# Two graph attention layers on one core: norms split by token tile, weigh placed ahead of scores, probability scalings on ScalarE

## The chip, the cores and the metric

The kernel runs on one core of a Trainium2 chip. A core has five engines that matter here, each with a queue of its own: TensorE (PE) multiplies matrices, VectorE (DVE) and ScalarE (ACT) work element by element and can read PSUM, GpSimd (POOL) works element by element in SBUF, and SyncE (SP) issues transfers. The metric is device time in microseconds (us) of one execution. Three runs of the kernel before took 3923.49 to 3931.69 us, with a median of 3928.25.

## The reference

There are 64 graphs of 256 nodes with 512 features, and a boolean adjacency matrix for each. Two layers follow each other; all arithmetic is in fp32.

```
# layer 0, 4 heads of 64
h = relu(layernorm(x))
q, k, v = h @ Wq, h @ Wk, h @ Wv
p = softmax(where(adj, q k^T / 8, -max))
x = x + (p v) @ Wo + bo
# layer 1, 8 heads of 64, adjacency with the diagonal added
h = relu(layernorm(x))
h = layernorm(h) * gamma + beta
q, k, v = split(h @ w_qkv.T)
p = softmax(where(adj | eye, q k^T / 8, -1e9))
x = x + (p v) @ w_out.T + b_out
```

## The kernel before

One step (index s) handles two graphs, which are four tiles (t) of 128 tokens; there are 32 steps. A step passes through these functions:

- load_h brings x and the adjacency matrix in. norm0 takes mean and variance of each token tile on DVE (moments: L198, L199), the inverse root on POOL (L203, a power of -0.5 over all four tiles at once) and scales the rows on DVE (scale_rows, L208, one instruction a tile).
- transpose_h turns the normalised rows so that features lie on partitions (PE L252, four transposes a call, four calls c a layer), and copies them out of PSUM: on ACT for layer 0 (L256, with the relu), on DVE for layer 1 (L258, with gamma and beta). After the fourth call POOL forms sums of them (act_sums, L96 to L99).
- project_qk and project_v multiply by the weights (PE L325 and L347), combine multiplies by the output weights (PE L362). All three use a scheme of Strassen and Winograd: seven products instead of eight, called in the order 1, 6, 7, 5, 2, 4, 3. Products 2, 4 and 3 go on in the PSUM banks of products 1, 7 and 5, so these banks stay taken until late. Each product is taken out by ACT or DVE: evacuate (L269 to L281) for the projections, accumulate (L288 to L303) for combine. In accumulate, product 1 is copied to u by ACT (L288), and product 6 is added to u by DVE (L290).
- scores handles a pair of heads (pr) for both graphs: PE L386; then eight blocks of 128 x 256, in two groups of four, one for each graph g. In a group and for each of four blocks, DVE adds the mask and takes the extreme value (L396), and ACT takes the exponential with its sum (L402). After the four, DVE forms the reciprocals of the sums (L407), and the four blocks are scaled by them: those of the first head of the pair (e == 0) on DVE (L412), those of the second on ACT (L414).
- turn transposes the probabilities (PE L423) and copies them back, by DVE for the first head (L427) and by ACT for the second (L429).
- weigh multiplies them by v (PE L441); ACT copies the result into oT (L447), and after the last pair POOL forms its sums (act_sums).
- norm1 prepares layer 1: for each token tile moments, subtraction of the mean with relu (DVE L231), moments again and the addition of the output bias on POOL (L235). After the fourth tile come the variance terms (L237, L238), the inverse root on POOL (L203) and four L208.
- mask makes the additive mask from the adjacency bytes on POOL (L188; for layer 1 also two L192). The mask of layer 1 has one buffer, so a new one can only be written when the last scores of the step before have read the old one.

PSUM is split in two pools of four banks each: ps_sc for scores and turn, ps_mm for everything else.

Which work stands where is decided by a list of places. A step lasts 6 units of place, and what belongs to layer 0 of step s runs in the period two before that of its layer 1. So layer 0 of one step fills the gaps of layer 1 of another. The calls are sorted by place and made in that order:

```python
    def at(period, place, fn, *args):
        events.append((period * PERIOD + place * SET, len(events), fn, args))
```

PE keeps the order of the calls exactly (manual_schedule at L59). On the other engines the framework's scheduler orders the instructions when the program is built, with its own estimate of when each will be ready. When they run, each engine takes its queue in order. The buffers of a pool are given out when the program is built, too.

In the steady state, the part of a period that the following sections speak of runs like this on PE: scores of layer 1, pair 1; product 1 of combine of layer 0 (another step); weigh of pair 2; two transposes of layer 0 (L252); product 6 of combine; two more transposes; the other five products of combine; turn of pair 1; products 1 and 6 of project_qk of layer 0; scores of pair 3; weigh of pair 1; products 7, 5, 2 and 4 of project_qk; turn of pair 3; product 3.

Of the kernel before, what the change touches and what calls it, by code (L numbers as in the profile page):

```python
# [8 lines left out]
FP = mybir.dt.float32  # L9
U8 = mybir.dt.uint8  # L10
AF = mybir.ActivationFunctionType
ALU = mybir.AluOpType

EPS = 1e-5
# [5 lines left out]
def kernel(  # L20
# [16 lines left out]
    nc = tc.nc  # L37
    P = 128
    B, N, D = x.shape
# [4 lines left out]
    NT = G * NIC  # L44
# [9 lines left out]
    act = ctx.enter_context(tc.tile_pool(name="act", bufs=1))  # L54
    sm = ctx.enter_context(tc.tile_pool(name="sm", bufs=2))
    stat = ctx.enter_context(tc.tile_pool(name="stat", bufs=4))
# [52 lines left out]
    bout_b = const.tile([P, D], FP, name="bout_b")  # L109
# [57 lines left out]
    S = [dict() for _ in range(NSTEP)]  # L167
# [28 lines left out]
    def moments(mv, src, t):  # L196
        bs = stat.tile([P, 6], FP, name="bs")
        nc.vector.bn_stats(bs, src[:, t, :])  # L198
        nc.vector.bn_aggr(mv[:, t, :], bs)  # L199

    def rsqrt(var, name):
        r = stat.tile([P, NT], FP, name=name, bufs=2)
        nc.gpsimd.tensor_tensor(r, var, mhalf, ALU.pow)  # L203
        return r

    def scale_rows(h, mean, r):
        for t in range(NT):
            nc.vector.tensor_scalar(  # L208
                h[:, t, :], h[:, t, :], mean[:, t, 0:1], r[:, t:t + 1],
                op0=ALU.subtract, op1=ALU.mult,  # L210
            )

    def norm0(s):
        h = S[s]["h"]
        mv = stat.tile([P, NT, 2], FP, name="mv0", bufs=2)
        for t in range(NT):
            moments(mv, h, t)
        ve = stat.tile([P, NT], FP, name="ve0", bufs=2)
        nc.vector.tensor_scalar(ve, mv[:, :, 1], EPS, None, op0=ALU.add)
        scale_rows(h, mv, rsqrt(ve, "r0"))  # L220

    def norm1(s):
        st, x1 = S[s], S[s]["xt"]
        mv = stat.tile([P, NT, 2], FP, name="mv1", bufs=2)
        mg = stat.tile([P, NT, 2], FP, name="mg", bufs=2)
        h = st["h"] = act.tile([P, NT, D], FP, name="h")
        for t in range(NT):
            moments(mv, x1, t)  # L230
            nc.vector.tensor_scalar(  # L231
                h[:, t, :], x1[:, t, :], mv[:, t, 0:1], 0.0, op0=ALU.subtract, op1=ALU.max
            )
            moments(mg, h, t)
            nc.gpsimd.tensor_tensor(x1[:, t, :], x1[:, t, :], bout_b, ALU.add)  # L235
        ve = stat.tile([P, NT], FP, name="ve1", bufs=2)
        nc.vector.tensor_scalar(ve, mv[:, :, 1], EPS, EPS, op0=ALU.add, op1=ALU.mult)  # L237
        nc.vector.tensor_tensor(ve, ve, mg[:, :, 1], ALU.add)  # L238
        scale_rows(h, mg, rsqrt(ve, "r1"))


    def blocks_of(b, pairs):
# [134 lines left out]
    def scores(s, lyr, pr):  # L377
        st = S[s]
        qk, neg = st.pop(("qk", lyr, pr)), st[f"n{lyr}"]
        sc = {h: ps_sc.tile([P, NIC, N], FP, name="sc") for h in HEADS}  # L380
        for g in range(G):
            for ic in range(NIC):
                for e in range(2):
                    rows = slice(e * DH, (e + 1) * DH)
                    i0 = g * N + ic * P
                    nc.tensor.matmul(  # L386
                        sc[g, e][:, ic, :], qk[rows, 0, i0:i0 + P],
                        qk[rows, 1, g * N:(g + 1) * N], start=True, stop=True,
                    )
        pm = {h: sm.tile([P, NIC, N], FP, name="pm", bufs=8) for h in HEADS}  # L390
        sa = stat.tile([P, 3, G, 2, NIC], FP, name="sa", bufs=2)
        for g in range(G):
            for e in range(2):
                for ic in range(NIC):

                    nc.vector.tensor_tensor_reduce(  # L396
                        out=pm[g, e][:, ic, :], in0=sc[g, e][:, ic, :],
                        in1=neg[:, g * NIC + ic, :],
                        scale=-SCALE, scalar=SMAX, op0=ALU.add, op1=ALU.min,
                        accum_out=sa[:, 0, g, e, ic:ic + 1],  # L400
                    )
                    nc.scalar.activation(  # L402
                        pm[g, e][:, ic, :], pm[g, e][:, ic, :], AF.Exp,
                        bias=sa[:, 0, g, e, ic:ic + 1], scale=-1.0,
                        accum_out=sa[:, 1, g, e, ic:ic + 1],
                    )
            nc.vector.reciprocal(sa[:, 2, g], sa[:, 1, g])  # L407
            for e in range(2):
                for ic in range(NIC):
                    pv, inv = pm[g, e][:, ic, :], sa[:, 2, g, e, ic:ic + 1]  # L410
                    if e == 0:
                        nc.vector.tensor_scalar(pv, pv, inv, None, op0=ALU.mult)  # L412
                    else:
                        nc.scalar.activation(pv, pv, AF.Copy, scale=inv)  # L414
        st["pm", lyr, pr] = pm

    def turn(s, lyr, pr):
# [42 lines left out]
    def at(period, place, fn, *args):  # L460
        events.append((period * PERIOD + place * SET, len(events), fn, args))

    def at_set(period, place, share, fn, *args):
        for i, n in enumerate((1, 6, 7, 5, 2, 4, 3)):
            at(period, place + i * share / 7, fn, *args, n)

    for s in range(NSTEP):

        p = s - 2
        at(p - 1, 5.6, load_h, s)  # L470
        at(p, 1.0, norm0, s)
        at(p, 2.9, mask, s, 0)
        for c in range(NC):
            at(p, 3.03 + 0.03 * c, transpose_h, s, 0, c)
        at_set(p, 3.5, 1.0, project_qk, s, 0, 0)
        at_set(p, 4.5, 0.5, project_v, s, 0)
        at(p, 4.5, scores, s, 0, 0)
        at(p, 5.15, turn, s, 0, 0)
        at(p, 5.6, scores, s, 0, 1)
        at(p, 5.601, weigh, s, 0, 0, True, False)  # L480
        at(p, 6.3, turn, s, 0, 1)
        at(p, 7.001, weigh, s, 0, 1, False, True)
        at(p, 7.4, load_x, s)
        at(p, 8.6, first_bias, s)
        at_set(p, 9.0, 0.5, combine, s, 0)
        at(p, 9.5, norm1, s)

        p = s
        for c in range(NC):
            at(p, -0.85 + 0.15 * c, transpose_h, s, 1, c)  # L490
        at(p, 0.3, mask, s, 1)
        at_set(p, 0.0, 1.0, project_qk, s, 1, 0)
        at_set(p, 1.0, 1.0, project_v, s, 1)
        at_set(p, 2.0, 1.0, project_qk, s, 1, 1)
        at(p, 1.0, scores, s, 1, 0)
        at(p, 1.65, turn, s, 1, 0)
        at(p, 2.0, scores, s, 1, 2)
        at(p, 2.001, weigh, s, 1, 0, True, False)
        at(p, 2.65, turn, s, 1, 2)
        at(p, 3.0, scores, s, 1, 1)  # L500
        at(p, 3.001, weigh, s, 1, 2, False, False)
        at(p, 3.5, turn, s, 1, 1)
        at(p, 3.75, scores, s, 1, 3)
        at(p, 3.751, weigh, s, 1, 1, False, False)
        at(p, 4.25, turn, s, 1, 3)
        at(p, 4.501, weigh, s, 1, 3, False, True)
        at_set(p, 5.0, 1.0, combine, s, 1)
        at(p, 6.0, store, s)

# [38 lines left out]
```

## Time and profile before

| | |
|---|---|
| median of three runs | 3928.25 us |
| profiled execution | 3926.11 us |
| its span, first to last instruction | 3924.3 us |
| mean granted clock of PE | 0.978 |
| PE busy | 3665.1 us, 93% |
| DVE busy | 2517.4 us, 64% |
| ACT busy | 1690.2 us, 43% |
| POOL busy | 1385.1 us, 35% |
| L412, scaling on DVE | 768 instructions, 354.6 us, mean 501 ns |
| L414, scaling on ACT | 768 instructions, 345.6 us, mean 498 ns |
| L402, exponential on ACT | 1536 instructions, 760.9 us, mean 496 ns |
| L396, masking on DVE | 1536 instructions, 563.1 us, mean 416 ns |

A row of the groups names line, engine and operation, then what is written from what, and how often; behind it stand the busy time, the mean duration, and the idle time of the engine just before, with what ended it. Durations overlap: the next instruction of a kind may start before the one before it has ended, so the pitch from start to start can be shorter than the mean. PE's matmuls in fp32 appear as two records each. A busy share says little about the end of the kernel, except for the engine that is nearly always busy; for the others the waits tell which of their results came late.

### The profile page before, as it was taken

The numbers are of one execution on the slowest core, as the hardware profiler recorded it, in microseconds if no ns is written. First come the engines' busy times: TensorE is split into PE (matmuls) and PEld (weight loads), VectorE is DVE, ScalarE is ACT, GpSimd is POOL, SyncE is SP. The second block draws the span as 40 slices with busy tenths as digits, with TensorE's granted clock in tenths as the row PEclk, the third lists the DMA queues.
The fourth block names the chain that finished last, engine by engine and source line by source line (L and its number), as shares of the span: only waits on it lengthen the run. The fifth ranks groups of instructions, "written<-read, shape, count | busy, mean of one in ns | idle before, by whom it ended". The sixth has DMA issues, their size and how long they took to land.

```text
span 3924.3 us, 59006 instructions
## 1 busy us (share of the span) xinstructions
PE 3665.1 (93%) x21953; PEld 3039.7 (77%) x21953; DVE 2517.4 (64%) x7193; ACT 1690.2 (43%) x4945; POOL 1385.1 (35%) x1170
## 2 busy tenths in 40 slices
PE   5999999999999999999999999999999999999988
PEld 4787778877778877788777878777887778787767
DVE  5666666666666666656666666666566666666654
ACT  2444444444444344444444443444444444444443
POOL 4244333343332433333433324333334333243331
PEclk9999999999999999999999999999999999999999
DMA  3000000010000100100000001101010000010000
GB/s 118 12 34 34 6 31 33 34 35 21 16 33 34 34 34 2 34 33 34 34 13 24 33 34 34 34 2 34 33 35 34 13 24 33 35 34 33 1 22 22
DMA packets 74127, 115.45 MB, mean 29 GB/s; under 512 B 18792, under 2 KB 22384, under 8 KB 73840
## 3 DMA queue, kind: packets, MB, share of 16 engines
q1 hardware_dynamic: 67584, 104.87, 7.8%
q10 hardware_dynamic: 6256, 6.82, 0.6%
q8 instruction: 172, 2.82, 0.3%
q14 instruction: 115, 0.94, 0.1%
HBM read 78.12 MB, written 33.55 MB: 28 GB/s over the span
## 4 chain that ended last, share of the span: by engine, by line
PE 70%; DVE 16%; ACT 9%; POOL 2%; issue 2%; DMA 1%; ACTq 0%; DVEq 0%; POOLq 0%
PE mm L325 23%; PE mm L362 14%; PE mm L347 13%; PE sc L423 7%; PE sc L386 7%; ACT pm L402 6%; PE mm L441 5%; DVE bs L198 4%; DVE pm L396 3%; PE mm L252 3%; ACT pm L414 2%; DVE h L231 2%; DVE pm L412 2%; DVE h L208 2%; DVE pm L427 1%
## 5 line engine op out<-in xcount | busy, mean ns | idle before, releaser
L325 PE MATMUL mm<-hT,wqkv 128*128 128x256 f32 x5376 | 1236.8, 385 | 112.9 <-DVE qk L273 100.0
L325 PEld LDWEIGHTS mm<-hT,wqkv 128*128 128x128 f32 x5376 | 1015.2, 192 | 281.8 <-issue 138.5
L402 ACT ACTIVATE pm<-pm,sa 128x256 f32<-128x256 f32 x1536 | 760.9, 496 | 706.1 <-DVE sa L396 701.9
L362 PE MATMUL mm<-wo,oT 128*128 128x256 f32 x2688 | 655.0, 393 | 91.4 <-ACT oT L447 72.2
L396 DVE CUSTOM_DVE_ANT_0 pm<-sc,n 128x256 f32<-128x256 f32 x1536 | 563.1, 416 | 188.5 <-PE sc L386 186.0
L362 PEld LDWEIGHTS mm<-wo,oT 128*128 128x128 f32 x2688 | 503.7, 196 | 187.3 <-issue 91.3
L347 PE MATMUL mm<-wqkv,hT 128*128 128x128 f32 (+1 forms) x3584 | 627.7, 330 | 6.8 <-DVE v L273 4.7
L347 PEld LDWEIGHTS mm<-wqkv,hT 128*128 128x128 f32 x3584 | 545.2, 191 | 81.7 <-issue 24.5
L291 POOL TENSOR_TENSOR xt<-xt,u 128x512 f32<-128x512 f32 x64 | 81.3, 1271 | 1120.2 <-DVE u L290 1120.2
L429 ACT COPY pm<-sc 128x512 f32<-128x512 f32 x384 | 225.1, 586 | 505.2 <-PE sc L423 505.2
L423 PE MATMUL sc<-ident,pm 128*128 128x128 f32 x3072 | 385.4, 279 | 17.8 <-DVE pm L412 17.7
L423 PEld LDWEIGHTS sc<-ident,pm 128*128 128x128 f32 x3072 | 360.3, 145 | 43.2 <-DVE pm L412 23.7
L386 PE MATMUL sc<-qk 64*128 64x256 f32 x3072 | 384.0, 389 | 1.0 <-DVE qk L281 1.0
L441 PE MATMUL mm<-pm,v 128*64 128x256 f32 x3072 | 376.3, 387 | 0.0
L414 ACT ACTIVATE pm<-pm,sa 128x256 f32<-128x256 f32 x768 | 345.6, 498 | 58.5 <-DVE sa L407 58.5
L412 DVE TENSOR_SCALAR pm<-pm,sa 128x256 f32<-128x256 f32 x768 | 354.6, 501 | 5.8
L386 PEld LDWEIGHTS sc<-qk 64*128 64x128 f32 x3072 | 278.6, 186 | 80.7 <-issue 47.1
L427 DVE COPY pm<-sc 128x512 f32<-128x512 f32 x384 | 254.3, 685 | 116.3 <-PE sc L423 116.1
L441 PEld LDWEIGHTS mm<-pm,v 128*64 128x64 f32 x3072 | 204.4, 137 | 147.4 <-issue 54.9
L402 ACT ACTIVATION_READ_ACCUMULATOR pm<-pm,sa 128x1 f32 x1536 | 287.3, 187 | 0.0
L96 POOL TENSOR_TENSOR oT<-oT 128x512 f32<-128x512 f32 (+1 forms) x64 | 73.8, 1154 | 557.9 <-ACT oT L447 557.9
L184 POOL TENSOR_TENSOR xt<-xt,bo_b 128x512 f32<-128x512 f32 x128 | 161.5, 1292 | 254.8 <-DMA xt<-in_x_dram 254.8
(78 smaller groups left out, 3427.6 us busy)
## 6 DMA issues: line engine op xcount, KB each, us to landing
h<-in_x_dram SPq DMA_DIRECT2D x32, 1024.0 KB, 5.2
xt<-in_x_dram SPq DMA_DIRECT2D x32, 1024.0 KB, 5.1
out_dram<-xt SPq DMA_DIRECT2D x32, 1024.0 KB, 4.3
ad<-in_adj_dram SPq DMA_DIRECT2D x32, 128.0 KB, 2.2
wr<-in_L_gnn_w_qkv_dram ACTq DMA_DIRECT2D x3, 1024.0 KB, 8.7
wr<-in_L_gnn_w_out_dram ACTq DMA_DIRECT2D x1, 1024.0 KB, 9.6
wqkv<-in_L_gnn_Wq_dram ACTq DMA_DIRECT2D x4, 128.0 KB, 5.0
wqkv<-in_L_gnn_Wk_dram ACTq DMA_DIRECT2D x4, 128.0 KB, 4.1
```

What stands on the lines that cost most here:

```text
L325: nc.tensor.matmul(bank[:, k, :], w[:, wa, c, k, a * P:(a + 1) * P], st["hT"][:, ba, c, :], start=first and (k, c) == (0, 0), stop=(k, c) ...
L347: nc.tensor.matmul(bank[:, t, :], st["hT"][:, ba, c, t * P:(t + 1) * P], w[:, wa, c, 2, :], start=first and (t, c) == (0, 0), stop=(t, c) ...
L362: nc.tensor.matmul(bank[:, t, :], st[f"oT{lyr}"][:, ba, c, t * P:(t + 1) * P], w[:, wa, c, :], start=first and (t, c) == (0, 0), stop=(t, ...
L386: nc.tensor.matmul(sc[g, e][:, ic, :], qk[rows, 0, i0:i0 + P], qk[rows, 1, g * N:(g + 1) * N], start=True, stop=True,)
L396: nc.vector.tensor_tensor_reduce(out=pm[g, e][:, ic, :], in0=sc[g, e][:, ic, :], in1=neg[:, g * NIC + ic, :], scale=-SCALE, scalar=SMAX, o ...
L402: nc.scalar.activation(pm[g, e][:, ic, :], pm[g, e][:, ic, :], AF.Exp, bias=sa[:, 0, g, e, ic:ic + 1], scale=-1.0, accum_out=sa[:, 1, g, e ...
L412: nc.vector.tensor_scalar(pv, pv, inv, None, op0=ALU.mult)
L414: nc.scalar.activation(pv, pv, AF.Copy, scale=inv)
L423: nc.tensor.transpose(pp[:, jc, ic * P:(ic + 1) * P], pm[:, ic, jc * P:(jc + 1) * P], ident)
L427: nc.vector.tensor_copy(pm, pp)
L429: nc.scalar.copy(pm, pp)
L441: nc.tensor.matmul(po[e * DH:(e + 1) * DH, g, :], st[f"v{lyr}"][:, g * NIC + jc, c0:c0 + DH], pT[g, e][:, jc, :], start=(jc == 0), stop=(j ...
```

## The change

Three things change.

Norms come in pieces. scale_rows becomes scale_row, which handles one tile. norm0 and norm1 become functions of one tile, too; the call for the last tile also makes the variance terms and the inverse root. Each piece has a place of its own. norm0 stood at place 1.0 whole; its pieces stand at 0.4 to 1.6, and its scalings at 2.05 to 2.65. norm1 stood at 9.5 whole; its pieces stand at 9.5 to 10.25, its scalings at 10.5 to 10.8. The operations and their number are the same.

weigh is placed 0.001 ahead of the scores of the next unit, where it stood 0.001 behind them.

All scalings of probabilities run on ACT.

```diff
-    def scale_rows(h, mean, r):
-        for t in range(NT):
-            nc.vector.tensor_scalar(
-                h[:, t, :], h[:, t, :], mean[:, t, 0:1], r[:, t:t + 1],
-                op0=ALU.subtract, op1=ALU.mult,
-            )
+    def scale_row(s, t):
+        h, mean, r = S[s]["h"], S[s]["mean"], S[s]["r"]
+        nc.vector.tensor_scalar(
+            h[:, t, :], h[:, t, :], mean[:, t, 0:1], r[:, t:t + 1],
+            op0=ALU.subtract, op1=ALU.mult,
+        )
...
+    def norm1(s, t):
         st, x1 = S[s], S[s]["xt"]
...
+        moments(mv, x1, t)
+        nc.vector.tensor_scalar(
+            h[:, t, :], x1[:, t, :], mv[:, t, 0:1], 0.0, op0=ALU.subtract, op1=ALU.max
+        )
+        moments(mg, h, t)
+        nc.gpsimd.tensor_tensor(x1[:, t, :], x1[:, t, :], bout_b, ALU.add)
+        if t == NT - 1:
+            ve = stat.tile([P, NT], FP, name="ve1", bufs=2)
+            nc.vector.tensor_scalar(ve, mv[:, :, 1], EPS, EPS, op0=ALU.add, op1=ALU.mult)
+            nc.vector.tensor_tensor(ve, ve, mg[:, :, 1], ALU.add)
+            st["r"] = rsqrt(ve, "r1")
...
                     pv, inv = pm[g, e][:, ic, :], sa[:, 2, g, e, ic:ic + 1]
-                    if e == 0:
-                        nc.vector.tensor_scalar(pv, pv, inv, None, op0=ALU.mult)
-                    else:
-                        nc.scalar.activation(pv, pv, AF.Copy, scale=inv)
+                    nc.scalar.activation(pv, pv, AF.Copy, scale=inv)
...
-        at(p, 1.0, norm0, s)
+        for t in range(NT):
+            at(p, 0.4 + 0.4 * t, norm0, s, t)
+            at(p, 2.05 + 0.2 * t, scale_row, s, t)
...
-        at(p, 5.601, weigh, s, 0, 0, True, False)
+        at(p, 5.599, weigh, s, 0, 0, True, False)
...
-        at(p, 7.001, weigh, s, 0, 1, False, True)
+        at(p, 6.999, weigh, s, 0, 1, False, True)
...
-        at(p, 9.5, norm1, s)
+        for t in range(NT):
+            at(p, 9.5 + 0.25 * t, norm1, s, t)
+            at(p, 10.5 + 0.1 * t, scale_row, s, t)
...
-        at(p, 2.001, weigh, s, 1, 0, True, False)
+        at(p, 1.999, weigh, s, 1, 0, True, False)
...
-        at(p, 3.001, weigh, s, 1, 2, False, False)
+        at(p, 2.999, weigh, s, 1, 2, False, False)
...
-        at(p, 3.751, weigh, s, 1, 1, False, False)
+        at(p, 3.749, weigh, s, 1, 1, False, False)
...
-        at(p, 4.501, weigh, s, 1, 3, False, True)
+        at(p, 4.499, weigh, s, 1, 3, False, True)
```

The instructions of the built program can be listed engine by engine for both kernels. With the lines of the kernel before, around the part described above, they stand like this (ACT after the scores of pair 1, and POOL between the sums of hT and those of oT):

```
        before                                  changed
ACT     6 L402, 2 L414, 2 L402, L288,           L447, 6 L402, 4 L414, 2 L402,
        2 L414, L447, 4 L256                    L288, 4 L414, 4 L256
POOL    4 L235, L203, L188, 2 L192              3 L235, L188, L235, 2 L192, L203
```

On DVE, before, the maskings L396 of pair 3 are mixed with rows 2 and 3 of norm1. In the changed kernel all eight stand together behind three rows, ahead of the end of row 3, the copy L273, the variance terms and the four L208; the second reciprocal L407 stands behind the first L208.

More of the change, by code (lines that the diff above doesn't have):

```diff
@@ L204, in rsqrt @@
         return r
-    def scale_rows(h, mean, r):
-        for t in range(NT):
-            nc.vector.tensor_scalar(
-                h[:, t, :], h[:, t, :], mean[:, t, 0:1], r[:, t:t + 1],
-                op0=ALU.subtract, op1=ALU.mult,
-            )
[L213 to L220, printed above, removed]
@@ L224, in norm1 @@
-    def norm1(s):
-        st, x1 = S[s], S[s]["xt"]
[L226 to L239, printed above, removed]
+    def scale_row(s, t):
[4 more added lines that the diff above has]
+        )
@@ new lines, in norm0 @@
+    def norm0(s, t):
+        st = S[s]
+        if t == 0:
+            st["mean"] = stat.tile([P, NT, 2], FP, name="mv0", bufs=2)
+        moments(st["mean"], st["h"], t)
+        if t == NT - 1:
+            ve = stat.tile([P, NT], FP, name="ve0", bufs=2)
+            nc.vector.tensor_scalar(ve, st["mean"][:, :, 1], EPS, None, op0=ALU.add)
+            st["r"] = rsqrt(ve, "r0")
+    def norm1(s, t):
+        st, x1 = S[s], S[s]["xt"]
+        if t == 0:
+            st["mv"] = stat.tile([P, NT, 2], FP, name="mv1", bufs=2)
+            st["mean"] = stat.tile([P, NT, 2], FP, name="mg", bufs=2)
+            st["h"] = act.tile([P, NT, D], FP, name="h")
+        mv, mg, h = st["mv"], st["mean"], st["h"]
+        moments(mv, x1, t)
[4 more added lines that the diff above has]
+        nc.gpsimd.tensor_tensor(x1[:, t, :], x1[:, t, :], bout_b, ALU.add)
+        if t == NT - 1:
+            ve = stat.tile([P, NT], FP, name="ve1", bufs=2)
+            nc.vector.tensor_scalar(ve, mv[:, :, 1], EPS, EPS, op0=ALU.add, op1=ALU.mult)
+            nc.vector.tensor_tensor(ve, ve, mg[:, :, 1], ALU.add)
+            st["r"] = rsqrt(ve, "r1")
```

## The prediction

> **What bounds the kernel now.** I read the page first: TensorE (PE) is busy 93% of the span, VectorE (DVE) 64%, ScalarE (ACT) 43%, GpSimd (POOL) 35%. So only what makes PE idle, or slow, is worth anything. The waits of PE alone come next; the columns are total us, times, longest.
>
> ```profile
> PE mm L325 <- DVE qk L273: 100.0, 30, 3.6
> PE mm L362 <- ACT oT L447: 72.2, 30, 2.4
> PE mm L252 <- DVE h L208: 21.6, 3, 17.5
> PE mm L362 <- POOL oT L98: 17.8, 3, 12.2
> PE sc L423 <- DVE pm L412: 17.7, 21, 4.5
> ```
>
> Two waits come once in each of 30 steps: stall Q (3.3 us, in project_qk of layer 0) and stall C (2.4 us, in combine of layer 0). The rest belongs to start and end. From one stall C to the next it is 119.97 us on average ((3671.41 - 192.27) / 29, timeline). Then the windows view around one stall C; the seventh figure, behind the five engines, is the granted clock.
>
> ```profile
> 2112.50:2115.00 2.50, 0.09 (x2) 0.06 (x1) 0.79 (x3) 2.50 (x8) 0.00 (x0) 1.00 0.00 0
> 2115.00:2118.00 3.00, 3.00 (x10) 2.52 (x11) 0.69 (x1) 0.90 (x3) 0.12 (x1) 0.50 0.02 5
> ```
>
> After the stall PE runs at half clock for about 3.4 us and loses 1.7 us more. Taking a window of 12 us around each stall, 19 of 30 C and 16 of 30 Q show it: some 2.0 us per step. Without stalls a step would be 119.97 - 2.4 - 3.5 - 2.0 = 112.0 us (3.5 is Q with the 0.27 us that the turn behind it waits).
>
> What ends stall C is in ACT's timeline (start, us, operation), with PE's last:
>
> ```profile
> 2110.70 0.50 ACT L402 ACTIVATE pm<-pm,sa 128x256 f32<-128x256 f32 x1
> 2111.20 0.90 ACT L414 ACTIVATE pm<-pm,sa 128x256 f32<-128x256 f32 x2
> 2112.98 0.57 ACT L288 COPY u<-mm 128x512 f32<-128x512 f32 x1
> 2113.44 0.91 ACT L414 ACTIVATE pm<-pm,sa 128x256 f32<-128x256 f32 x2
> 2114.25 0.57 ACT L447 COPY oT<-mm 128x512 f32<-128x512 f32 x1
> 2114.72 1.08 ACT L256 ACTIVATE hT<-mm 128x512 f32<-128x512 f32 x2
> ...
> 2114.97 2.04 PE L362 MATMUL mm<-wo,oT 128*128 128x256 f32 x4 [2.41 <-ACT oT L447]
> ```
>
> The second product of combine needs a PSUM bank of ps_mm (four of them). The one it gets was filled by weigh, whose copy L447 stands behind a whole softmax unit in ACT's queue: exps at a pitch of 0.49 us, scalings at 0.40 (two take 2111.20 to 2111.99). Note L256 right behind: the copies of the transposes free the next two banks. Stall Q, in the same way, from DVE, PE and POOL:
>
> ```profile
> 2017.69 1.91 DVE L208 TENSOR_SCALAR h<-h,mg,r 128x512 f32<-128x512 f32 x4 [0.91 <-POOL r L203]
> 2020.20 0.69 DVE L273 TENSOR_TENSOR qk<-mm,qk 128x512 f32<-128x512 f32 x1
> ...
> 2021.04 1.97 PE L325 MATMUL mm<-hT,wqkv 128*128 128x256 f32 x8 [3.48 <-DVE qk L273]
> ...
> 2016.60 1.06 POOL L203 TENSOR_TENSOR r<-ve,mhalf 128x4 f32<-128x4 f32 x1 [0.55 <-DVE ve L238]
> 2020.38 1.04 POOL L188 TENSOR_SCALAR n<-ad 128x1024 f32<-128x1024 uint8 x1 [2.72 <-DVE sa L396]
> 2021.51 2.55 POOL L192 TENSOR_TENSOR n<-n,offdiag 128x512 f32<-128x512 f32 x2
> ```
>
> The copy L273 waits in DVE's queue behind norm1; the inverse root L203 runs ahead of the mask (L188, L192), which has to wait for the last masking L396 of the unit.
>
> [...] a gap of 2.4 us is enough here, and one of 3.48 us (at 2021.04) was followed by full clock; so I take it by chance per stall. [...] L447 above had its matmuls done at 2111.47 and went at 2114.25. [...] two L231 took 1.37 us beside POOL at 2005.75, one alone 0.49.
>
> **Part 1, scalings.** 768 DVE instructions of 501 ns (L412) go, 768 of ACT at a pitch of 0.40 us come. PE waits for neither as a sum. What counts is a unit's tail on ACT: exps start 1.63 us after the scores start (2106.60 to 2108.23), then 8 x 0.49 + 8 x 0.40 = 7.1: done at 8.8 instead of 7.2. Four products (7.0) or more stand between scores (1.93) and turn in every unit, so turn comes at 8.9 or later and asks for the second group's first head at 9.8. Hidden, by 1 us, as long as nothing delays the exps.
>
> **Part 2, weigh ahead of scores.** The same 16 matmul passes (1.88 us) 1.93 us earlier. Its operands, the turn's copies, are ready: two to four products lie between. Its own copy L447 now goes before the exps. So the bank of stall C is free in time, and the wait is gone. What is late next: the built instruction order shows that the third transpose now waits for DVE. The other three banks are held by the first product and by two transposes, so it takes the second product's bank. That is emptied by L290, which needs the copy L288, which in ACT's order now stands as: 6 exps, 4 scalings, 2 exps, L288, 4 scalings, then all four L256.
>
> From the start of the scores, in us: exps 1.63 to 4.60, scalings to 6.18, exps to 7.17, L288 ends 7.74, L290 (0.69) ends 8.55. PE: scores 1.93, product 1.06, transposes 1.04, product 0.9: ready for the third transpose at 4.9, starts at 8.65. The fourth needs the first L256: scalings 7.63 to 9.22, L256 ends 9.8, so it starts at 9.9; its end, 10.4, meets the second L256 (10.3). Sum: 10.4 against 5.9 without waits. **Stall C becomes 4.5 us instead of 2.4.** Bounds: 4.0 (both handoffs immediate) to 4.8.
>
> **Part 3, norms in pieces.** norm0's rows come out 2 us earlier than before, since two pairs of L412 are gone from between them (L219 at 2060.78, 11.1 us after its scores start, becomes some 8.6), and nothing waited for them in the steady steps. norm1 is nearly at its old place on DVE: the order still has two and a half of its rows behind the turn's copies, but now ahead of the maskings L396. POOL's order is the news: L188, the last L235, both L192, and only then L203. The inverse root queues behind the mask, which waits for the unit's last L396. Behind the first L208, which waits for it on DVE, stand the second reciprocal L407, three L208 and two copies; ACT's scalings of the second group wait for L407, and turn for them.
>
> From the start of turn (2003.01 above): PE turn 1.74, two products 3.55, weigh 1.88: scores at 7.17, fourth later product wanted at 7.17 + 1.93 + 5.3 = 14.4. DVE: copies end 2.6; then three L231 (0.5), six L198 (0.6) and one evacuation L271 (0.65), with 0.5 for five aggregates and 0.4 of lockout by POOL's L297: 6.6, to 9.2; eight L396 at 0.345 plus reciprocal to 12.4. POOL: L188 12.5 to 13.55. L231 of row 3 is shut out by it until 13.55, ends 14.0; L273 ends 14.7, so PE waits 0.4 there. POOL goes on: L235 to 15.35, two L192 to 17.9, L203 to 18.95. DVE: L208 19.05, L407 at 19.5 to 19.7; scalings of one head at 20.55, of the next 21.35. PE, with turn's first two heads done at 17.4, waits to 20.65 and then 0.35 more. **Stall Q becomes 4.0 us instead of 3.5**, with another name: turn waiting for ACT L414. Bounds: 2.5 (no lockout, L396 without delay) to 4.3.
>
> **Clock.** [...] half clock should follow nearly every C and some 6 of 10 Q; part of a C window falls into the 0.8 us that remain. 0.95 x 1.4 + 0.6 x 1.7 = 2.4 us against 2.0; between 1.6 and 3.2.
>
> **Ends.** In the last step nothing fills PE between scores and turn. There weigh no longer covers the wait (1.9 us), and turn's last head comes at 9.2 + 0.5; the two last units (3881.40 to 3898.78, 17.4 us) come to 1.9 + 9.7 + 2.5 + 9.7 = 23.8: +6.4. The start gets one more addition L184 (1.27) ahead of the 12.2 us wait for L98: +1.
>
> **Sum.** Per step (4.5 - 2.4) + (4.0 - 3.5) + (2.4 - 2.0) = +3.0; times 30 = 90, plus 7: +97. The profiled execution took 3926.11 (span 3924.30), so 4023; the median of the runs is 2 higher. I say 4020. With the bounds, a step gains between about 1.0 and 4.2: 3960 to 4060.
>
> **Rivals.**
> 1. Q goes, C grows (chance 0.08): if the inverse root isn't late, 3.5 becomes 0.4 and a clock loss of 1.0 goes; with C's 2.1, a step is 2 us shorter: about 3875. For it: DVE loses 354.6 us of L412. Against: POOL's order.
> 2. It does what it says (0.03): both stalls gone, 112 us a step: 3926 - 30 x 8 + 7 = 3693. This is the faster side; it decides only if the third transpose gets another bank than the second product's and L203 runs ahead of the mask. Both orders speak against it.
> 3. Break-even within 0.2% (0.04): Q at its low bound and C at 4.0 with fewer half-clock windows.
> 4. A third stall (0.13): the 1 us of cover in part 1 is used up where DVE or ACT starts a unit late; 1 us in two units of each step gives 4080.
> The forecast has 0.72.
>
> **From these to the numbers.** 3960 to 4060 holds the forecast's range and the near edge of rival 4; rivals 1 and 2 are left out. About 0.2% (8 us) is what a measurement can tell from no change. Faster 0.11 (rivals 1 and 2), same 0.04, slower 0.85.
>
> **What would show it.** In the profile after: PE L423 waiting some 3 us for ACT L414 once a step; PE L252 (the transposes) waiting 3.7 us for DVE L290 and 0.8 for L256; L407 idle behind L208; L203 after L192 on POOL; no wait for L447. A step of about 123 us. I am wrong if turn doesn't wait in its second group, or if the transposes run through.

## The result, and the profile after

The changed kernel takes 4023.1 us (median of four runs, 4020.74 to 4026.86) against 3925.93 in the runs of the kernel before beside them: ratio 1.0246, 95% interval 1.0228 to 1.0264. Its profiled execution took 4020.74 us, with a span of 4018.9 and a mean granted clock of 0.968 (before: 3926.11, 3924.3 and 0.978).

Lines of the changed kernel from scores on are three higher than before: L399 masks, L405 is the exponential, L410 the reciprocal, L291 and L293 take out products 1 and 6 of combine. L412 is gone, L414 has the same number. The first row of the page before, then of the page after, and the waits of PE after (total us, times, longest):

```profile
PE 3665.1 (93%) x21953; PEld 3039.7 (77%) x21953; DVE 2517.4 (64%) x7193; ACT 1690.2 (43%) x4945; POOL 1385.1 (35%) x1170
...
PE 3732.3 (93%) x21953; PEld 3055.0 (76%) x21953; DVE 2225.7 (55%) x6425; ACT 2004.1 (50%) x5713; POOL 1368.6 (34%) x1170
```

```profile
PE mm L255 <- DVE u L293: 111.6, 30, 3.7
PE sc L423 <- ACT pm L414: 88.0, 36, 3.5
...
PE mm L255 <- ACT hT L259: 21.2, 30, 0.7
```

Read the two rows against each other. The count of PE's instructions is the same, 21953, but they take 3732.3 us instead of 3665.1. So 67 of the 94.6 us that the span has grown lie in PE's busy time and not in its gaps. The trace also records every change of the granted clock, which is 1.00 or 0.50, and this clock record explains most of them: half of PE's busy time inside the stretches of half clock is 74 us before and 116 us after, 42 more. The gaps explain only the rest. Their names are those that the prediction gave: the third transpose waits for L293 (stall C), the fourth for L259, and turn waits for L414 (stall Q).

Stall C in the timelines of ACT, DVE and PE (start, us, operation; in brackets the wait ahead of it):

```profile
2036.24 1.69 ACT L414 ACTIVATE pm<-pm,sa 128x256 f32<-128x256 f32 x4
...
2038.81 0.56 ACT L291 COPY u<-mm 128x512 f32<-128x512 f32 x1
2039.28 1.70 ACT L414 ACTIVATE pm<-pm,sa 128x256 f32<-128x256 f32 x4
2040.88 1.53 ACT L259 ACTIVATE hT<-mm 128x512 f32<-128x512 f32 x3
...
2039.40 0.69 DVE L293 TENSOR_TENSOR u<-mm,u 128x512 f32<-128x512 f32 x1 [0.29 <-ACT u L291]
...
2040.15 0.66 PE L255 MATMUL mm<-ident,h 128*128 128x128 f32 x4 [3.72 <-DVE u L293]
2041.51 1.11 PE L255 MATMUL mm<-ident,h 128*128 128x128 f32 x4 [0.70 <-ACT hT L259]
```

Product 1 was done by 2034.7, but its copy L291 stands behind four scalings and two more exponentials. Stall Q, from POOL, DVE, ACT and PE:

```profile
2062.87 2.50 POOL L192 TENSOR_TENSOR n<-n,offdiag 128x512 f32<-128x512 f32 x2
2065.32 1.02 POOL L203 TENSOR_TENSOR r<-ve,mhalf 128x4 f32<-128x4 f32 x1
...
2066.38 0.55 DVE L208 TENSOR_SCALAR h<-h,mg,r 128x512 f32<-128x512 f32 x1 [1.62 <-POOL r L203]
2066.84 0.17 DVE L410 RECIPROCAL sa<-sa 128x4 f32<-128x4 f32 x1
...
2067.04 1.71 ACT L414 ACTIVATE pm<-pm,sa 128x256 f32<-128x256 f32 x4 [3.87 <-DVE sa L410]
...
2067.60 2.10 PE L423 MATMUL sc<-ident,pm 128*128 128x128 f32 x8 [2.47 <-ACT pm L414]
```

The end of one late root on POOL (2066.34) passes through DVE and ACT to PE within 1.3 us. Then the windows view around both stalls, cut where the clock's record changes and 3.41 us before that; the figure after the length of a stretch is PE's busy time, the seventh is the granted clock:

```profile
2037.82:2041.23 3.41, 0.66 (x4) 0.42 (x4) 0.87 (x2) 3.41 (x11) 1.06 (x1) 1.00 0.00 0
2041.23:2044.65 3.42, 3.14 (x10) 2.69 (x11) 0.22 (x1) 1.78 (x4) 2.71 (x3) 0.50 0.00 0
...
2065.13:2068.54 3.41, 0.87 (x6) 0.59 (x5) 2.17 (x6) 1.50 (x4) 1.21 (x2) 1.00 0.00 0
2068.54:2071.95 3.41, 3.40 (x11) 2.70 (x10) 1.61 (x3) 1.75 (x4) 0.00 (x0) 0.50 0.01 2
```

Each of the two stalls is followed by a stretch of half clock, in which PE is busy nearly all the time (3.14 of 3.42 us, 3.40 of 3.41). And the steps have become strangely regular. From one stall C to the next it is 122.88 us, to within 0.01, in every step from the fifth on; before, it changed between 119.46 and 121.82. 122.88 is 36 times 3.413 us, and 3.413 us is the length of a stretch of half clock in these traces: from 400 to 3600 us, each of 52 in the changed kernel lasts that long, and 31 of 32 before (the other lasts twice as long). In the clock records of both kernels all stretches of half clock, but for the last ones, which the end of a trace cuts off, last whole multiples of 3.413 us, and in each of the two traces they begin on one grid of that length, to within 0.01 us. The experiments show that this is no accident. A piece of that grid, 3.413 us long, is called a window below.

### The profile page after: what moved, and what is told of

It is laid out like the page before. It is cut to its first block, busy times and chain, and to the rows that moved or that the text cites. A ratio compares the mean times of both kernels' runs of the same rounds, so it can differ in the third digit from the quotient of the medians.

```text
span 4018.9 us, 59244 instructions
## 1 busy us (share of the span) xinstructions
PE 3732.3 (93%) x21953; PEld 3055.0 (76%) x21953; DVE 2225.7 (55%) x6425; ACT 2004.1 (50%) x5713; POOL 1368.6 (34%) x1170
## 4 chain that ended last, share of the span: by engine, by line
PE 76%; ACT 9%; DVE 8%; POOL 5%; issue 1%; DMA 0%; ACTq 0%; POOLq 0%; DVEq 0%
PE mm L328 22%; PE mm L350 15%; PE mm L365 14%; PE sc L423 8%; PE mm L441 8%; PE sc L389 7%; ACT pm L405 5%; ACT pm L414 3%; DVE bs L198 3%; PE mm L255 2%; DVE h L233 2%; POOL n L192 2%; POOL xt L237 1%; DVE pm L399 1%; POOL r L203 1%
## 5 line engine op out<-in xcount | busy, mean ns | idle before, releaser
L328 PE MATMUL mm<-hT,wqkv 128*128 128x256 f32 x5376 | 1257.0, 390 | 10.4 <-POOL hT L98 8.8
L328 PEld LDWEIGHTS mm<-hT,wqkv 128*128 128x128 f32 x5376 | 1033.1, 196 | 190.5 <-issue 43.0
L405 ACT ACTIVATE pm<-pm,sa 128x256 f32<-128x256 f32 x1536 | 758.6, 495 | 232.2 <-DVE sa L399 232.2
L399 DVE CUSTOM_DVE_ANT_0 pm<-sc,n 128x256 f32<-128x256 f32 x1536 | 553.4, 417 | 453.6 <-PE sc L389 453.6
L414 ACT ACTIVATE pm<-pm,sa 128x256 f32<-128x256 f32 x1536 | 651.9, 495 | 171.3 <-DVE sa L410 171.3
L365 PE MATMUL mm<-wo,oT 128*128 128x256 f32 x2688 | 663.7, 397 | 18.4 <-POOL oT L98 16.2
L365 PEld LDWEIGHTS mm<-wo,oT 128*128 128x128 f32 x2688 | 518.3, 201 | 107.7 <-issue 21.4
L447 ACT COPY oT<-mm 128x512 f32<-128x512 f32 x192 | 112.6, 586 | 899.4 <-PE mm L441 899.4
L423 PE MATMUL sc<-ident,pm 128*128 128x128 f32 x3072 | 409.7, 283 | 90.7 <-ACT pm L414 88.0
L441 PE MATMUL mm<-pm,v 128*64 128x256 f32 x3072 | 377.8, 388 | 1.3 <-DVE pm L427 1.3
L441 PEld LDWEIGHTS mm<-pm,v 128*64 128x64 f32 x3072 | 202.8, 138 | 152.1 <-issue 55.6
L255 PE MATMUL mm<-ident,h 128*128 128x128 f32 x1024 | 170.0, 299 | 154.6 <-DVE u L293 111.6
L405 ACT ACTIVATION_READ_ACCUMULATOR pm<-pm,sa 128x1 f32 x1536 | 286.8, 187 | 0.0
L255 PEld LDWEIGHTS mm<-ident,h 128*128 128x128 f32 x1024 | 129.4, 152 | 199.4 <-DVE u L293 123.6
```

The lines of the kernel that those rows point to most:

```text
L255: nc.tensor.transpose(pv[:, t * P:(t + 1) * P], st["h"][:, t, c * P:(c + 1) * P], ident)
L328: nc.tensor.matmul(bank[:, k, :], w[:, wa, c, k, a * P:(a + 1) * P], st["hT"][:, ba, c, :], start=first and (k, c) == (0, 0), stop=(k, c) ...
L365: nc.tensor.matmul(bank[:, t, :], st[f"oT{lyr}"][:, ba, c, t * P:(t + 1) * P], w[:, wa, c, :], start=first and (t, c) == (0, 0), stop=(t, ...
L399: nc.vector.tensor_tensor_reduce(out=pm[g, e][:, ic, :], in0=sc[g, e][:, ic, :], in1=neg[:, g * NIC + ic, :], scale=-SCALE, scalar=SMAX, o ...
L405: nc.scalar.activation(pm[g, e][:, ic, :], pm[g, e][:, ic, :], AF.Exp, bias=sa[:, 0, g, e, ic:ic + 1], scale=-1.0, accum_out=sa[:, 1, g, e ...
L423: nc.tensor.transpose(pp[:, jc, ic * P:(ic + 1) * P], pm[:, ic, jc * P:(jc + 1) * P], ident)
```

## The experiments

All times are medians, the ratio is to runs of the kernel before that were taken beside them, and the last four columns are us per step, read from PE's timeline and the windows view of the stretch from 400 to 3600 us. "Busy" is PE's share of that stretch times the step, "waits" the rest. The last column is the price of half clock: half of PE's busy time inside the stretches of half clock, summed from the trace's clock record. (In them the matmuls of L328 and L365 follow each other at 427 ns instead of 216, and the transposes at 213 instead of 109, so half of the time is lost.) Busy less half clock is not the same everywhere: 111.7 us before, 112.7 in the changed kernel, 113.0 at most (the dose runs aside). A short wait can hide in it, since a transpose's record lasts 0.27 us where the next one starts 0.11 us later. Runs with one edit start from the kernel named in their text.

| run | us | ratio (95%) | step | waits | busy | half clock |
|---|---|---|---|---|---|---|
| before | 3925.93 | | 119.97 | 6.2 | 113.8 | 2.1 |
| changed | 4023.1 | 1.0246 (1.0228 to 1.0264) | 122.88 | 7.0 | 115.9 | 3.3 |
| scalings_alone | 4115.3 | 1.0484 (1.0461 to 1.0507) | 126.29 | 9.3 | 117.0 | 5.3 |
| weigh_alone | 4026.5 | 1.0255 (1.0232 to 1.0278) | 122.89 | 7.0 | 115.9 | 3.8 |
| norms_whole | 4026.33 | 1.0257 (1.0230 to 1.0284) | 122.88 | 6.2 | 116.7 | 4.7 |
| weigh_behind | 3921.96 | 0.9988 (0.9973 to 1.0003) | 119.47 | 5.9 | 113.6 | 1.7 |
| root_first | 3950.89 | 1.0054 (1.0038 to 1.0070) | 120.32 | 5.6 | 114.8 | 2.2 |
| reciprocal_first | 3943.96 | 1.0050 (1.0031 to 1.0070) | 120.30 | 5.4 | 114.9 | 2.2 |
| copies_on_vector | 3876.14 | 0.9864 (0.9845 to 0.9883) | 118.19 | 4.1 | 114.1 | 1.1 |
| both_mended | 3817.01 | 0.9715 (0.9699 to 0.9732) | 116.05 | 2.5 | 113.6 | 0.6 |
| three_orders | 3816.56 | 0.9730 (0.9711 to 0.9748) | 116.08 | 3.0 | 113.1 | 0.4 |
| rows_behind_turn | 3742.79 | 0.9528 (0.9502 to 0.9554) | 113.56 | 0.9 | 112.7 | 0 |
| dose_08_after | 4026.47 | 1.0247 (1.0230 to 1.0263) | 122.88 | 6.5 | 116.4 | 3.2 |
| dose_16_after | 4079.87 | 1.0399 (1.0380 to 1.0418) | 124.59 | 6.6 | 118.0 | 3.9 |

### Which part of the change costs what

**scalings_alone**: the kernel before, with its scalings on ACT.

```diff
-                    if e == 0:
-                        nc.vector.tensor_scalar(pv, pv, inv, None, op0=ALU.mult)
-                    else:
-                        nc.scalar.activation(pv, pv, AF.Copy, scale=inv)
+                    nc.scalar.activation(pv, pv, AF.Copy, scale=inv)
```

> The kernel before with one edit: all scalings of probabilities on ScalarE; norms whole, weigh behind scores. Theory A (my prediction's): stall C keeps its old form (product 6 of combine waits for weigh's copy L447), but that copy now stands behind two more scalings twice over, 4 x 0.40 = 1.6 us: C 4.0 instead of 2.4. The inverse root stays ahead of the mask on GpSimd, so stall Q keeps its old form (L325 waits for L273), about 3.2. With the half clock that follows both, a step of about 122.9 us instead of 119.97 and 4015 us in all (3985 to 4020): the scalings alone bring nearly all of the loss. Theory B (the order made by weigh and the norm pieces is what costs, ScalarE has room): 3926 us, C at 2.4.

Measured: 4115.3 us, more than any theory said, and more than the whole change costs. The waits of PE:

```profile
PE mm L325 <- DVE sa L407: 140.9, 30, 5.1
PE mm L362 <- ACT oT L444: 119.9, 30, 4.0
```

C is 4.00 as worked out, so the 1.6 us of extra scalings ahead of weigh's copy are shown. Q is 4.7 instead of the 3.2 expected. Its cause stands in the timelines of DVE and POOL:

```profile
2109.18 4.62 DVE L208 TENSOR_SCALAR h<-h,mg,r 128x512 f32<-128x512 f32 x4 [0.79 <-POOL r L203]
...
2109.23 1.05 POOL L188 TENSOR_SCALAR n<-ad 128x1024 f32<-128x1024 uint8 x1
2110.36 2.71 POOL L192 TENSOR_TENSOR n<-n,offdiag 128x512 f32<-128x512 f32 x2
```

Four L208 took 1.91 us in the kernel before. Here they take 4.62, with the mask beside them: all eight maskings now stand ahead of L208 on DVE, so nothing holds the mask back until the rows are scaled. Half of the loss is clock (5.3 us a step against 2.1): PE is idle for a part of the first window of half clock behind a stall (busy for 3.18 of the 3.50 us from 2086.00, at a clock of 0.50), and at both stalls half clock goes on into a second window (clock 0.62 from 2089.50 to 2093.00, 0.79 from 2118.00 to 2121.50).

**weigh_alone**: the kernel before, with all six calls of weigh ahead of the scores.

```diff
-        at(p, 2.001, weigh, s, 1, 0, True, False)
+        at(p, 1.999, weigh, s, 1, 0, True, False)
...
-        at(p, 4.501, weigh, s, 1, 3, False, True)
+        at(p, 4.499, weigh, s, 1, 3, False, True)
```

> The kernel before with one edit: weigh ahead of the next scores. Theory A: C takes its new form (third transpose waits for L290), but with only two scalings per group on ScalarE L288 ends 0.8 us earlier: 2.85 plus 0.15, so 3.0. The root stays ahead of the mask; L273 comes later on VectorE, because two L412, two L396 and L407 stand ahead of it: Q about 3.9. Step 121.9, in all 3983 us (3950 to 4010). Theory B: the whole loss is here, 4015 or more. Theory C (weigh ahead frees the bank and nothing comes late): C gone, 3860 or less.

Measured: 4026.5 us, steps of 122.5 and 123.2 in turn, 122.89 on average. C has its new form at 3.19 (3.0 expected), Q waits for L273 for 3.18 (3.9 expected), and project_v waits 0.60 more. The time is the one that theory B gave, but not for its reason, since the scalings alone cost still more.

**norms_whole**: the changed kernel, with the pieces of both norms at the old places.

```diff
...
-            at(p, 9.5 + 0.25 * t, norm1, s, t)
-            at(p, 10.5 + 0.1 * t, scale_row, s, t)
+            at(p, 9.5, norm1, s, t)
+        for t in range(NT):
+            at(p, 9.5, scale_row, s, t)
```

> The changed kernel with one part undone: norm0 and norm1 stand whole at their old places 1.0 and 9.5; weigh ahead and scalings on ScalarE stay. Theory A: the pieces' places do nothing, the order on VectorE and GpSimd around the mask is the same as in the changed kernel: 4023 us (4010 to 4030), C 4.4 and Q 2.5 as there. Theory B (the pieces made the root late): Q goes, 3880 us.

The time, 4026.33 us, is the one expected by theory A, but its reason is false. The trace has POOL's old order again: four L237, the root at 2059.43, the mask at 2063.23. So it is the pieces that put the root behind the mask. Q took its old form (L328 waits 2.23 us for L276). The waits are 0.8 us a step shorter than in the changed kernel, half clock costs 1.4 more, the rest of PE's busy time is 0.6 shorter, and the step is the same 122.88.

**weigh_behind**: the changed kernel, with weigh behind the scores again (the reverse of the diff of weigh_alone).

> The changed kernel with one part undone: weigh behind the next scores, as before; norm pieces and scalings on ScalarE stay. Theory A: C in its old form at 4.0 us (weigh's copy behind eight scalings of its unit less four, as in the scalings-alone run). The root is even later on GpSimd (last of all, behind the mask and the fourth addition), but here the reciprocal of the second group stands ahead of the four L208 on VectorE, so ScalarE's scalings and turn don't wait for the root: Q gone. 112 + 4.0 + 1.7 = 117.7 us a step, 3860 us (3840 to 3920): faster than before. Theory B (the late root itself costs): Q 2.5 or more stays, 4000 us or more.

Measured: 3921.96 us, no difference from before that these runs could tell. The mechanism came as expected: C 4.00, and the wait for the scalings of turn is gone although the root is last on POOL. But a wait of 1.06 us for L410 and two of 0.4 are left. These 1.9 us are what the expected 117.7 us lack: the step is 119.47, to within 0.02, from the third on. That is 35 windows.

These four and the two kernels make a table in which parts don't add. The pieces take 193 us off scalings_alone (to 3922), but nothing off norms_whole (to 4023). weigh ahead takes 89 off scalings_alone and adds 101 to weigh_behind. The differences between 3922, 4024 and 4115 are 102 and 91 us, and the steps are 35, 36 and 37 windows. Such a table alone doesn't show a lock, since one edit can also change the waits that another leaves; the next two runs leave the waits' causes as they are.

### Does time add up? A dose of work

The changed kernel, with some transposes of turn done twice, which changes no value; the order on DVE, ACT and POOL is the same.

```diff
+                    for _ in range(1 + ((lyr, pr) == (1, 0) and g == 0)):
                         nc.tensor.transpose(
                             pp[:, jc, ic * P:(ic + 1) * P], pm[:, ic, jc * P:(jc + 1) * P], ident
                         )
```

dose_08_after has this for one graph (8 transposes of 0.11 us a step), dose_16_after for both.

> The changed kernel with 8 more transposes of 0.11 us a step: turn of layer 1's pair 0 transposes the first graph's probabilities twice, which changes nothing in the result; the order on the other engines is unchanged. It measures whether time adds up. Parts add: +0.9 us a step, 4050 us. Lock: the step stays at 36 windows and the half-clock loss falls by 0.9, 4023 us as before the edit; or, if there is no room, it goes to 37 windows, 4125 us.

> The changed kernel with 16 more transposes of 0.11 us a step (turn of layer 1's pair 0 done twice for both graphs), order of the other engines unchanged. With 8 more, the time did not move (4026.5 against 4023.1). Lock with room left: 36 windows again, 4026 us. Room used up: up to 37 windows, 4125 us; parts adding from here on: 4050 us.

0.88 us of work a step, 28 us in all, cost no more than 3 us. The steps of dose_08_after begin at 123.58, 124.88, 123.80, 123.11, 122.97 and 122.90 us and settle at 122.88. The dose is paid back at the two stalls. The waits of PE, then the third and fourth transposes of one step:

```profile
PE mm L255 <- DVE u L293: 111.6, 30, 3.7
PE sc L424 <- ACT pm L414: 87.5, 36, 3.3
...
PE mm L255 <- ACT hT L259: 8.4, 30, 0.7
```

```profile
2045.09 1.11 PE L255 MATMUL mm<-ident,h 128*128 128x128 f32 x4 [3.72 <-DVE u L293]
2046.44 1.11 PE L255 MATMUL mm<-ident,h 128*128 128x128 f32 x4 [0.24 <-ACT hT L259]
```

In the changed kernel the half clock began at 2041.23, 1.08 us after the third transposes had started (2040.15). Here it begins at 2044.96, 0.13 us before they start, so that they take 1.11 us instead of 0.66. But the fourth have to wait for L259 anyway: their wait falls from 0.70 to 0.24, and less of the combine behind them runs at half clock. From the third transposes to turn it is 7.09 us instead of 7.69. At stall Q the half clock also begins sooner (0.32 us after turn goes on, instead of 0.94), where turn is held up by ACT's scalings, and 0.29 us are saved. Together that is 0.89, the dose. The price of half clock as such hardly changes (3.3 to 3.2).

The double dose broke this lock: steps of 123.74 and 125.44 in turn, a mean of 124.59. That is 73 windows in two steps, and 57 us more in all. None of the three figures expected for it was met.

So in these runs a step which draws half clock mostly settles at a whole number of windows, or at one over two steps; root_first and reciprocal_first repeat every four steps (141 windows), both_mended takes 102 windows for three. copies_on_vector, with 34.63 windows a step, fits no such ratio, and the kernel before reaches 119.46 (35 windows) only in its last steps.

Behind which stalls half clock comes can be read from the traces of the two kernels, cut along the grid of the clock, from 400 to 3600 us. In the changed kernel the window ahead of each of the 52 stretches of half clock had 0.65 to 0.88 us of PE's work in it, in the kernel before the window ahead of each of the 32 had 0.57 to 1.54 us. So where a stall falls against the grid counts here, and not only its length. One stall Q of the kernel before, 3.48 us long, fell across two windows, with 1.56 and 1.78 us of work, and drew nothing:

```profile
2015.99:2019.41 3.42, 1.56 (x8) 1.03 (x6) 2.51 (x10) 1.29 (x5) 1.12 (x2) 1.00 0.00 0
2019.41:2022.82 3.41, 1.78 (x8) 1.58 (x9) 3.27 (x9) 2.47 (x7) 2.36 (x3) 1.00 0.07 18
2022.82:2026.23 3.41, 3.14 (x23) 2.75 (x22) 3.18 (x5) 1.17 (x2) 1.24 (x1) 1.00 0.09 21
```

In the changed kernel it is 2.47 us, falls into one window (0.87 us of work), and draws half clock in every step. For the lock's cause there is an estimate from these figures and from dose_08_after: a step that is a little long lets the half clock begin earlier against its stall, where it falls on work that would wait anyway, and so gets shorter. The first steps of dose_08_after fit this; that the other locks come about in the same way is not shown.

### Stall by stall

**root_first**: the changed kernel, with the mask ordered behind the root on POOL. issue_after sets the order in an engine's queue and adds no wait; ROOT holds the inverse root.

```diff
-        at(p, 0.3, mask, s, 1)
+        at(p, 0.3, mask_behind_root, s)
...
+    def mask_behind_root(s):
+        with tc.issue_after(ROOT["r1"].ins):
+            mask(s, 1)
```

> The changed kernel with one issue order added: on GpSimd the layer-1 mask (L188, two L192) must follow the inverse root L203 of norm1; the order on VectorE, ScalarE and TensorE is unchanged. Theory A (stall Q comes from the root behind the mask): L203 can start near 2062.8 of the profile's time instead of 2065.3, the second reciprocal and the scalings follow 2.5 us earlier, and turn doesn't wait: Q under 0.4 instead of 2.5. C stays at 3.7 and 0.7. Summing the parts: 112 + 4.4 + 1.7 + 0.2 = 118.3 us a step, 3886 us. Theory A with the lock that the first runs show (steady steps of 35, 36 or 37 clock windows of 3.413 us, whatever the parts): 35 windows, 119.47 us, 3921 us. Theory B (turn would wait for something else anyway): Q 2 us or more, 4023.

The root began at 2029.77, right after the variance terms, and turn waited 0.67 us, with 0.4 more at weigh. So the late root was the cause of most of stall Q. In the remainder the mask is beside DVE again: it now runs beside the first L208 (1.37 us instead of 0.55), behind which the reciprocal stands. The step is 120.32 us: two stalls that still draw half clock.

**reciprocal_first**: the changed kernel, with the other link of that chain cut: on DVE, norm1's rows come behind the second reciprocal of pair 3, which RECIP holds. POOL keeps the root last.

```diff
-            at(p, 10.5 + 0.1 * t, scale_row, s, t)
+            at(p, 10.5 + 0.1 * t, scale_row_behind, s, t)
...
+        last = RECIP.get((1, 3, 1))
...
+        with tc.issue_after(last.ins):
+            scale_row(s, t)
```

> The changed kernel with one other issue order: on VectorE the four L208 of norm1 must follow the second reciprocal of layer 1's pair 3; GpSimd's order (root last, behind the mask) is as in the changed kernel. Theory A (turn waits because the reciprocal stands behind an L208 that waits for the root): turn's wait for ScalarE is gone, though the root is as late as before. The copies of turn now come behind four late L208, so weigh may wait up to 1.2 us for them. Sum 112 + 4.4 + 1.7 + 1.2 = 119.3 us a step, 3917 us. Theory B (ScalarE itself is late there): the 2.5 us stay, 4023.

Of the 2.47 us 0.3 are left at turn, and 0.65 come at weigh: theory A. Both cuts lead to the same time within 7 us, and both lie above the sum of the parts (3886 and 3917).

**copies_on_vector**: the changed kernel, with stall C's copies on DVE.

```diff
-            nc.scalar.copy(u, bank)
+            nc.vector.tensor_copy(u, bank)
...
-            nc.scalar.activation(dst, ph, AF.Relu)
+            nc.vector.tensor_scalar(dst, ph, 0.0, None, op0=ALU.max)
```

> The changed kernel with two copies moved from ScalarE to VectorE: product 1 of combine into u (L291), and the relu copies of layer 0's transposes (L259). Theory A (C is the wait behind ScalarE's scalings): product 1 is copied at about 4.2 us after the scores start, product 6 is added at 5.65, the third transpose waits 0.8 instead of 3.7 and the fourth not at all. Q stays at 2.5. Sum 112 + 0.8 + 2.5 + 1.7 = 117 us a step, 3847 us; with the lock, 34 or 35 windows: 3818 or 3921. Theory B (VectorE is as late there as ScalarE): C stays above 2.5, 3980 us or more.

C falls from 4.4 to 0.70 us, at the fourth transpose instead of the third; Q stays at 2.47, and L276 adds 0.82. The step is 118.19: C was ACT's queue.

**both_mended**: root_first and copies_on_vector together.

> The changed kernel with both edits: the layer-1 mask behind the inverse root on GpSimd, and the two copies on VectorE. Theory A: C 0.8, Q under 0.4, no gap long enough for half clock: about 113 us a step, 3727 us (3700 to 3780), faster than both kernels by 5%. With half clock still once a step and the lock, 34 windows: 3818. Theory B (other results come late as soon as these two don't): 3900 or more.

3817.01 us, the second figure: 0.70 at C, 1.25 at turn, some half clock, 34.0 windows on average. **three_orders** adds the order of reciprocal_first:

> The both-mended kernel with the second reciprocal of layer 1's pair 3 ahead of the four L208 as well. In both-mended 1.25 us of stall Q were left, because the first L208 ran 1.37 us beside GpSimd's mask and the reciprocal stood behind it. Theory A: Q goes to 0, the 0.7 us for the fourth transpose stay, no half clock in the steady steps: 113 us a step, 3724 us (3700 to 3760). Theory L (any short wait still draws one half-clock window and the step locks to a whole number of windows): 34 windows, 3817 us as both-mended.

Nothing gained, and here is where it went (waits of PE, then DVE's timeline; lines are higher by the helpers that are added: L214 is the row scaling, L441 turn's copy):

```profile
PE mm L455 <- DVE pm L441: 62.3, 31, 2.1
PE mm L268 <- DVE hT L272: 20.9, 30, 0.7
```

```profile
1842.80 4.65 DVE L214 TENSOR_SCALAR h<-h,mg,r 128x512 f32<-128x512 f32 x4 [0.23 <-POOL r L209]
1847.37 0.68 DVE L295 TENSOR_TENSOR qk<-mm,qk 128x512 f32<-128x512 f32 x1
1847.97 1.27 DVE L441 COPY pm<-sc 128x512 f32<-128x512 f32 x2
```

The four rows stand ahead of turn's copies, and with the mask beside them they take 4.65 us instead of 1.91. The wait went from turn to the weigh behind it. **rows_behind_turn** starts from both_mended and puts the rows behind turn's copies of pair 3, the last of which LAST holds:

```diff
+        last = LAST.get((1, 3))
...
+        with tc.issue_after(last.ins):
+            scale_row(s, t)
```

> The both-mended kernel with the four L208 of norm1 put behind turn's copies L427 on VectorE, so that the reciprocal, the product's copy and turn's copies all come ahead of them. In three-orders the wait had only moved: 2.06 us of weigh for L427, behind the four L208. PE works 112.8 us a step at full clock there (115.67 less 0.70 and 2.06). Theory A (with the rows out of the way nothing is late): only the 0.7 us for the fourth transpose stay, 113.5 us a step and no half clock: 3740 us (3730 to 3760). Theory L (one half-clock window per step is drawn by the 0.7 us, and the steps lock to 34 windows): 3817 us again.

```profile
PE mm L268 <- DVE hT L272: 20.9, 30, 0.7
PE mm L268 <- DVE h L214: 19.5, 3, 16.4
PE mm L378 <- POOL oT L98: 17.5, 3, 10.8
```

```profile
400.00:3600.00 3200.00, 3175.45 (x19278) 2608.51 (x19274) 2041.72 (x5783) 1671.91 (x4847) 1190.78 (x1006) 1.00 0.09 29
```

3742.79 us against 3740 worked out, 4.7% below the kernel before and 7% below the changed one. The first wait comes once a step, the other two three times in all. The clock is 1.00, a step is 113.56 us, 33.27 windows, and all steps are alike to 0.02: without half clock there is no lock, and here the parts add up.

## Why the prediction was right

The time (4020 against 4023.1) and the sign were right, the two new waits were named rightly, and two of the sizes in the sum were wrong. (The sum itself, with the 2 us between profile and median, gives 4025, not 4020.)

- **Part 2, stall C.** Said 3.7 for the third transpose and 0.8 for the fourth; measured 3.72 and 0.70. copies_on_vector shows that ACT's queue makes it.
- **Part 3, stall Q.** The chain from the root to turn is as said, and root_first and reciprocal_first cut it at two links. The size was off: a gap of 2.47 us instead of 4.0. The 0.4 for L273 was not there: row 3's L233, which took 1.22 us beside POOL's L188 where one alone takes 0.49, ended in time. The gap in turn, 3.25, became 2.47, since turn goes on after one scaled block instead of two (0.4) and POOL reached the root 0.45 us earlier. Part of this comes back without a gap: the eight transposes then take 2.10 us, partly at ACT's pace of 0.40 us from one scaled block to the next, where 0.11 is usual. About 0.5 us a step is added in turn in this way.
- **Clock.** Said 2.4 us, up by 0.4; measured 3.3, up by 1.2. The start was right: 2.0 was said for the kernel before, and its clock record gives 2.1. The step that failed is "I take it by chance per stall", and with it the shares of 0.95 for C and 0.6 for Q, which were an estimate. In a locked step each stall falls on the same place of the clock's grid every time (the half clock begins 1.07 to 1.09 us after the third transposes in 28 of 30 steps), and both stalls draw their window in all 30. Before, stalls C of the same 2.40 us drew it 20 times in 30.
- **Part 1, scalings.** "Hidden" holds for PE's own wait, since no unit but that of stall Q waits for a scaling. But scalings_alone shows what the prediction didn't say: on the old order this edit alone costs 188 us, through the copy behind it (C 4.00) and the mask that it lets loose (Q 4.7).
- **Ends.** Said 7 us; the span grew by 94.6, of which 30 x 2.91 = 87.3 lie in the steps, so 7.3.

The errors nearly cancel, and that is luck: gaps grew by 0.8 us a step where 2.6 were said, half clock by 1.2 where 0.4 was said, and the rest of PE's busy time by 1.0 where nothing was said; 2.9 against 3.0. Half of that last term is turn's; where the other half comes from is open. One reading was off: a single L231, not two, took 1.37 us beside POOL, where one alone took 0.49. It ended at 2007.11, 0.28 us after POOL's L297 had (2006.83): what part 3 calls lockout. The lock helped: weigh_alone and norms_whole come to the same 36 windows with other waits, and the dose shows that 0.9 us a step more or less in the sum need not show in the time. So the time alone confirms little of the sum; the waits do. Of the rivals, the first (Q goes, 3875) is what root_first tried: 3951.

## What to carry to other kernels

Compare PE's busy time at an equal number of instructions before looking at waits: where it grows, sum the half clock from the clock's record (42 of 67 us here), and look for short waits in the rest. A wait can cost more than its length: behind stall Q of the changed kernel, 2.47 us, half clock took 1.7 us more. If a loop's period stays the same to 0.01 us, look whether it is a multiple of the length of a stretch of half clock (3.413 us here); then small gains and losses may not show, and single edits may not add up, until the last wait that draws half clock is gone. When moving work from one engine to another, look at which small instruction stands behind it in the queue, and which operation on a third engine it had been holding back.

## What the runs showed of the hardware

- A gap of 2.47 us (0.87 us of work in the 3.41 us ahead of the half clock) drew half clock in each of 30 steps of the changed kernel. One of 3.48 us before (1.56 and 1.78 us of work in 3.42 and 3.41 us) did not, and one of 0.70 us in a step of 113.56 never did in rows_behind_turn. In the steady steps half clock came in stretches of 3.41 or 6.83 us; one of 3.41 cost up to 1.7 us.
- Most steps that drew half clock locked to whole multiples of its stretch: 119.47, 122.88 and 126.29 us are 35, 36 and 37 times 3.413. 0.88 us of added work a step disappeared in such a lock, while 1.76 cost 1.71.
- A DVE tensor_scalar of 128 x 512 in fp32 came every 0.48 us without POOL beside it, and four took 4.62 to 4.65 us beside the mask, against 1.91.
